# A transformer block with 64 experts: the last two tiles of tokens are handled apart behind the attention, and the last tile's rows go behind each expert's first 128 places

## The chip, the cores and the metric

One core of a Trainium2 chip runs the whole program in one launch. The metric is the time of the program on the device in microseconds (us). Times below come from one profiled execution unless they are called medians.

## The reference

All numbers are float32. 2 sequences of 512 tokens with 256 features (1024 tokens in all) go through attention and a layer of experts, each followed by a layer norm over the sum with its input:

```python
qkv = x @ Wqkv.T + b_qkv                     # 16 heads of 16
scores = einsum('bqhd,bkhd->bhqk', q, k) / 4 + alibi_bias; causal mask; p = softmax(scores)
x = layernorm(x + (p @ v) @ Wout.T + b_out)
...
probs = softmax(x @ gate_w.T)                # 64 experts
topk_w, topk_idx = top_k(probs, 8); topk_w /= topk_w.sum()
a = silu(x @ w1[e]) * (x @ w3[e])            # 256 -> 96
y = sum over the 8 chosen e of topk_w * (a @ w2[e])
x = layernorm(x + y)
```

Each token goes to 8 of 64 experts, so there are 8192 pairs of token and expert, 128 to an expert on average.

## The kernel before

**Attention.** The 1024 tokens are 8 tiles of 128 (4 to a sequence, numbered 0 to 3 by their query positions). They are worked on in four blocks of two tiles: `blocks_` lists sequence 0 tiles 0 and 1, sequence 0 tiles 2 and 3, sequence 1 tiles 2 and 3, sequence 1 tiles 0 and 1. A written-out loop goes over `step`; a step takes two heads. In it stand the scores of these heads (`scores`, L318 on PE, with the row's extreme on DVE, L324), the exponentials of the heads of three steps before (`exponentials`: products L369 on PE, Exp on ACT L379, and on POOL the triangle `affine_select` L384), and in every second step the products with the values (`values`, L406 on PE). A block takes 8 steps. The order on PE, DVE and ACT is the order in which the loop writes instructions. On POOL, selects and scatters are chained in order of issue by `in_order`.

**Small jobs.** When a block's last values are done, its remaining work is spread over the following steps, one job a step: `normalize` for each of its two tiles, `turn_context`, `project` (L455), `norm` with `turn_x1`, `route` (gate products L505, top 8 by L516 and L517), `weigh` (weights into columns of x1, L551) with `find_places` (L561 to L580: running counts `seen` by products with a triangle and with ones, then places). `find_places` gives every pair of token and expert a row in the table `xg` in HBM: expert e owns 288 rows from e*288, and the pair goes to the first free one.

**Scatters.** `dispatch` then issues 16 indirect DMAs on POOL for a block (L587), each of 128 rows of 329 floats, with `at(step + 8 + m // (8 if end else 1), dispatch, s, 2 * m, 2 * m + 2)`: two scatters a step from the eighth step on, and for the last block all at once.

**Experts.** After all 64 scatters (`after_scatters`), rows come back from `xg` by SP (L793) as 128-row jobs: 64 "one" jobs (an expert's first 128 places), 16 "four" jobs (places 128 to 159 of four experts, four DMAs), 8 "pair" jobs (two halves of 64 further places, found from the counts). The order is: a four, two ones, a pair every second time, two ones, and so on. A job turns the rows (L799 on PE, L801 on DVE), makes gate and up products (L810), Silu (L818), the weighted product (L820), turns it (L825, L827), makes the down product (L834), copies it to one of 10 buffers `y` (L842), and scatters it by POOL to `results` in HBM (L849). Rows are loaded 8 jobs ahead and more, into 18 buffers. Lists for all that (counts, places, which expert a row of a four belongs to) are worked out on DVE behind the last `find_places` (L697 to L787).

**Weights.** Two experts' weights are one DMA of 640 KB (L106). 9 pairs are loaded at the start, 10 during the attention, 4 behind it (`lates`), and the last 9 into the places of the first 9, each as soon as its two ones are done.

**The rare loop.** If the 288 places or the 8 pairs don't suffice, a loop (L899) of up to 64 turns handles what is left over, ahead of the jobs. With these inputs it makes no turn, but each engine loads its count (L896), branches and meets the others.

**End.** When all results are written, SP loads them (L995, 8 MB), PE and DVE add each token's 8 rows, and the last norm and the output follow.

Of the kernel before, what the change touches and what calls it, by code (L numbers as in the profile page):

```python
# [48 lines left out]
def block_kernel(ctx: ExitStack, tc: tile.TileContext, x, wqk, wv, bqk, slope, bv, wo, bo, gate, wall, out):  # L49
# [179 lines left out]
    with tc.tile_pool(name="ps_s", bufs=4, space=PSUM) as ps_s, tc.tile_pool(  # L229
# [5 lines left out]
        blocks_ = [(0, 0), (0, 1), (1, 1), (1, 0)]  # L235
# [67 lines left out]
        def maxima_of(s, g):  # L303
            h = blocks_[s][1]
            return maxima[h][(sum(other == h for _, other in blocks_[:s]) * NG + g) % 3]

        def scores(u, a):

            s, g, js = heads_of(u)
            b, h = blocks_[s]  # L310
            q = 2 * h + a
# [10 lines left out]
            for j, ps in zip(js, pss):  # L322
                junk = sm.tile([P, S], F32, tag="neg", name=f"neg{u}_{a}_{j}", bufs=2)
                nc.vector.tensor_tensor_reduce(  # L324
                    out=junk[:, :n],
                    in0=ps[:, :n],
                    in1=mask[:, S - n :],
                    scale=-1.0,
                    scalar=BIG,
                    op0=ALU.add,  # L330
                    op1=ALU.min,
                    accum_out=m[:, a, j * HP + HD + 1 : j * HP + HD + 2],
                )
# [3 lines left out]
        def lower(s, g):  # L337

            b, h = blocks_[s]
            m = maxima_of(s, g)  # L340
            pm = small
            for a in range(2):
                nc.tensor.transpose(pm[:, a * P : (a + 1) * P], m[:, a, :], ident)
            ql = sm.tile([P, W2], F32, tag="ql", name=f"ql{s}_{g}", bufs=3)
            nc.vector.tensor_tensor(ql, pm, qT[b][:, g, h * W2 : (h + 1) * W2], ALU.add)
# [4 lines left out]
        def parts_of(h):  # L350

            parts = []
            for k in range(0, 2 * h, 2):
                parts.append([(k, 0, 0), (k + 1, 0, W2)])
            parts.append([(2 * h, 0, 0), (2 * h + 1, P, W2)])
            return parts

        def exponentials(u, part):

            s, g, js = heads_of(u)  # L360
            b, h = blocks_[s]
            ql = lowered[s, g]
            todo = parts_of(h)[part]
            last = part == h
            pts = [ps_t.tile([P, S], F32, tag="pt", name=f"pt{u}_{part}_{n}") for n in range(2)]
            for k, first, col in todo:
                for n, j in enumerate(js):
                    r = slice(j * HP, (j + 1) * HP)
                    nc.tensor.matmul(  # L369
                        pts[n][:, col : col + W2 - first],  # L370
                        lhsT=kT[b][r, g, k * P : (k + 1) * P],
                        rhs=ql[r, first:],
# [3 lines left out]
            cols = W2 + P if last else S  # L376
# [21 lines left out]
        def values(s, g):  # L398
            b, h = blocks_[s]
            pc = halves[:, 0, :]  # L400
            u = s * NPAIR + 2 * g
            prs = [[probs.pop((u + j // 2, part, j % 2)) for part in range(h + 1)] for j in range(4)]
            for part, todo in enumerate(parts_of(h)):
                for k, first, col in todo:
                    for j in range(4):
# [3 lines left out]
                            rhs=prs[j][part][:, col : col + W2 - first],  # L409
                            start=(k == 0),  # L410
                            stop=(k == 2 * h + 1),
# [3 lines left out]
            nc.scalar.copy(raw[s][:, g, :], pc)  # L415
# [3 lines left out]
        def normalize(s, a):  # L419

            pm = ps_s.tile([P, S], F32, tag="ps", name=f"pcn{s}_{a}")
            for g in range(NG):
                nc.tensor.transpose(pm[:, g * P : (g + 1) * P], raw[s][:, g, a * P : (a + 1) * P], ident)
# [12 lines left out]
        def turn_context(s):  # L436
            pm = ps_s.tile([P, S], F32, tag="ps", name=f"pcT{s}")
            for a in range(2):
# [5 lines left out]
            nc.scalar.copy(ctxT[s].rearrange("p a d -> p (a d)"), pm)  # L444

        def first_of(s):
            b, h = blocks_[s]
            return b * NQ + 2 * h

        def project(s):  # L450
            i = first_of(s)
            pm = ps_s.tile([P, S], F32, tag="ps", name=f"po{s}")
            for a in range(2):
# [8 lines left out]
            mine = x1[:, i : i + 2, :D]  # L462
            nc.vector.tensor_tensor(mine, pm.rearrange("p (a d) -> p a d", d=D), mine, ALU.add)
            mv = means[s] = st.tile([P, 2, 2], F32, tag="mv", name=f"mv{s}")
            for a in range(2):
# [3 lines left out]
            roots[s] = st.tile([P, 2], F32, tag="rstd", name=f"rstd{s}")  # L469
            nc.scalar.activation(roots[s], mv[:, :, 1], AF.Sqrt, bias=eps_s)  # L470

        def norm(s):
            i = first_of(s)
            mv, r = means[s], roots[s]
            nc.vector.reciprocal(r, r)
            shift = st.tile([P, 2], F32, tag="shift", name=f"shift{s}")
            nc.vector.scalar_tensor_tensor(shift, mv[:, :, 0], -1.0, r, ALU.mult, ALU.mult)
            for a in range(2):
# [4 lines left out]
                x1_d[i * P : (i + 2) * P, :].rearrange("(n p) d -> p n d", p=P), x1[:, i : i + 2, :D]  # L483
            )

        def turn_x1(s):
            i = first_of(s)
            pm = ps_s.tile([P, S], F32, tag="ps", name=f"px1T{s}")
            for c in range(DC):
                for a in range(2):  # L490
                    nc.tensor.transpose(
                        pm[:, c * W2 + a * P : c * W2 + (a + 1) * P], x1[:, i + a, c * P : (c + 1) * P], ident
                    )
            x1Ts[s] = st.tile([P, DC, W2], F32, tag="x1T", name=f"x1T{s}", bufs=1)
            nc.scalar.copy(x1Ts[s].rearrange("p c q -> p (c q)"), pm)

        scatters = []

        masks, tos, expd = {}, {}, {}

        def route(s):
            pm = small[:, : 2 * E].rearrange("p (a e) -> p a e", e=E)
            for a in range(2):
# [10 lines left out]
            rest = st.tile([P, 2, E], F32, tag="rest", name=f"rest{s}")  # L514
            for a in range(2):
# [3 lines left out]
                )  # L519
            least = st.tile([P, 2], F32, tag="least", name=f"least{s}")  # L520
            nc.vector.tensor_scalar(least, top[:, :, 0], -1.0, None, ALU.mult)
            masks[s] = st.tile([P, 2, E], F32, tag="mk", name=f"mk{s}")
            nc.vector.tensor_scalar(masks[s], rest, -BIG, None, ALU.is_equal)
            lg = st.tile([P, 2, E], F32, tag="lg", name=f"lg{s}")
            den = st.tile([P, 2], F32, tag="den", name=f"den{s}")
            for a in range(2):
# [5 lines left out]
        def weigh(s):  # L532
            i = first_of(s)
            lg, den = expd.pop(s)
            nc.vector.reciprocal(den, den)
            rest = st.tile([P, 2, E], F32, tag="rest", name=f"chosen{s}")
            den2 = st.tile([P, 2], F32, tag="den2", name=f"den2{s}")
            for a in range(2):
# [13 lines left out]
                x1[:, i : i + 2, D : D + E], rest, den2.unsqueeze(2).to_broadcast([P, 2, E]), ALU.mult  # L552
            )

        def find_places(s):

            i = first_of(s)
            mk = masks.pop(s)
            pm = small[:, : 2 * E].rearrange("p (a e) -> p a e", e=E)
            for a in range(2):  # L560
                nc.tensor.matmul(pm[:, a, :], lhsT=ones, rhs=seen, start=True, stop=False)  # L561
                if a:
                    nc.tensor.matmul(pm[:, a, :], lhsT=ones, rhs=mk[:, 0, :], start=False, stop=False)
                nc.tensor.matmul(pm[:, a, :], lhsT=before, rhs=mk[:, a, :], start=False, stop=True)
            mine = nth[:, i : i + 2, :]
            nc.vector.tensor_copy(mine, pm)
            for a in range(2):
                nc.vector.tensor_tensor(seen, seen, mk[:, a, :], ALU.add)


            place = st.tile([P, 2, E], F32, tag="place", name=f"place{s}")
            nc.vector.tensor_scalar(place, mine, float(CAP), float(1 << 16), ALU.is_ge, ALU.mult)
            nc.vector.tensor_tensor(place, place, mine, ALU.add)
            nc.vector.tensor_tensor(place, place, begin.unsqueeze(1).to_broadcast([P, 2, E]), ALU.add)
            nc.vector.tensor_tensor(place, place, mk, ALU.mult)
            p8 = x1[:, i : i + 2, D + E : D + E + TOPK]
            for a in range(2):
                nc.vector.max(out=p8[:, a, :], in_=place[:, a, :])
            tos[s] = const.tile([P, 2, TOPK], I32, name=f"to{s}")
            nc.vector.scalar_tensor_tensor(tos[s], p8, -1.0, beyond[:, i : i + 2, :], ALU.add, ALU.min)  # L580

        def dispatch(s, first, end):
            b, h = blocks_[s]
# [496 lines left out]
```

## Time and profile before

| | us |
|---|---|
| median of 6 runs | 458.31 (456.12 to 459.12) |
| the profiled execution, its own time | 461.04 |
| its span, first to last instruction | 459.3 |

| engine | busy us | share of the span |
|---|---|---|
| PE (products) | 354.4 | 77% |
| DVE | 234.7 | 51% |
| POOL | 201.0 | 44% |
| ACT | 163.0 | 35% |

| when (us) | what |
|---|---|
| 0 to 204 | attention, with the small jobs and scatters of the first blocks in between |
| 204 to 255 | small jobs and scatters of the last block, the lists |
| 256 to 425 | the 88 jobs of the experts |
| 426 to 459 | results are loaded and added, last norm, output |

A line of the profile gives start and length, or length and busy times, then the engine (PEld is PE's weight load, SPq and POOLq are queues that issue DMAs), the line of the code, the operation, output and input, and in brackets how long the engine was idle before and what released it. "DMA share" is the mean busy share of the core's 16 DMA engines. The granted clock is that of PE, as a share of full speed.

### The profile page before, as it was taken

The page shows a single profiled execution, that of the slowest core. Times are in us where ns is not written, and L with a number is a line of the kernel's source. Part 1 is how long each engine was busy: PE and PEld are TensorE (multiplying, and loading weights), DVE is VectorE, ACT ScalarE, POOL GpSimd, SP SyncE. Part 2 cuts the span into 40 slices and gives each one's busy share as a digit, 9 for nine tenths or more (in the row PEclk, how much of TensorE's full clock was granted, in tenths as well). Part 3 has the DMA queues.
Part 4 walks back from the last instruction along what each step waited for, and adds up shares of the span by engine and source line. Part 5 has one row for each costly group of instructions (what it writes and reads, how often), then busy time and mean ns, then how long its engine had stood idle before and what let it go on. Part 6 is the DMA issues. An engine that isn't in the chain of part 4 may idle for free. (4 is left out here: it accounts for less than half of the span.)

```text
span 459.3 us, 8458 instructions
## 1 busy us (share of the span) xinstructions
PE 354.4 (77%) x2546; PEld 233.1 (51%) x2546; DVE 234.7 (51%) x1040; ACT 163.0 (35%) x453; POOL 201.0 (44%) x278
## 2 busy tenths in 40 slices
PE   4399999997999789775200397889898799997493
PEld 2135544665666556453200266556666566765372
DVE  0825445763676247243291255546565556653285
ACT  2012332565445533624010144434444444545032
POOL 8911112111165418647567044545554565656000
PEclk9769999995899679857555599999999999999599
DMA  8999999999542203314833489987786667211793
GB/s 246 391 360 332 324 316 328 320 266 358 195 133 75 83 0 120 111 60 147 297 123 128 122 273 329 294 274 229 244 256 212 208 182 217 70 68 57 319 408 108
DMA packets 56591, 98.58 MB, mean 215 GB/s; under 512 B 7241, under 2 KB 40600, under 8 KB 55520
## 3 DMA queue, kind: packets, MB, share of 16 engines
q1 hardware_dynamic: 47728, 76.93, 52.7%
q0 software_dynamic: 7456, 19.46, 11.9%
q10 hardware_dynamic: 1360, 1.64, 1.1%
q8 instruction: 21, 0.34, 0.3%
q14 instruction: 26, 0.21, 0.2%
HBM read 52.38 MB, written 48.75 MB: 220 GB/s over the span
## 5 line engine op out<-in xcount | busy, mean ns | idle before, releaser
L849 POOL DMA_INDIRECT results<-y,rows x88 | 86.6, 984 | 84.8 <-DVE xT L801 29.4
L324 DVE CUSTOM_DVE_ANT_0 neg<-ps,mask 128x256 f32<-128x256 f32 (+3 forms) x128 | 57.4, 487 | 44.4 <-PE ps L318 38.3
L587 POOL DMA_INDIRECT xg<-x,to x64 | 63.7, 996 | 22.2 <-issue 16.7
L384 POOL TENSOR_SCALAR_AFFINE_SELECT pr<-pr 128x256 f32<-128x256 f32 x64 | 25.0, 408 | 110.4 <-ACT pr L379 110.3
L379 ACT ACTIVATE pr<-pt 128x384 f32<-128x384 f32 (+1 forms) x96 | 45.3, 523 | 45.9 <-PE pt L369 37.4
L799 PE MATMUL pxT<-ident,xb 128*128 128x128 f32 x176 | 36.2, 287 | 29.6 <-SPq L941 29.2
L801 DVE COPY xT<-pxT 128x256 f32<-128x256 f32 x88 | 37.1, 422 | 35.5 <-DMA xb<-xg 17.0
L799 PEld LDWEIGHTS pxT<-ident,xb 128*128 128x128 f32 x176 | 23.0, 144 | 46.7 <-issue 39.6
L818 ACT ACTIVATE s<-pg 128x96 f32<-128x96 f32 x88 | 22.2, 253 | 62.5 <-PE pg L810 31.8
L842 ACT COPY y<-py 128x256 f32<-128x256 f32 x88 | 32.8, 373 | 20.5 <-PE pxT L799 11.0
L810 PE MATMUL pg<-w,xT 128*32 128x192 f32 (+1 forms) x288 | 39.9, 345 | 0.3 <-issue 0.3
L825 PE MATMUL paT<-ident,a 128*96 128x128 f32 x88 | 25.9, 294 | 14.9 <-DVE a L820 11.3
L273 PE MATMUL pq<-room 128*128 128x512 f32 x64 | 35.3, 687 | 0.1
L369 PE MATMUL pt<-ql,kT 32*128 32x256 f32 (+1 forms) x192 | 32.1, 410 | 1.5 <-ACT pr L379 1.0
L318 PE MATMUL ps<-room 32*128 32x128 f32 (+3 forms) x128 | 26.9, 496 | 7.6 <-DVE room L279 7.6
L318 PE MATMUL ps<-kT,qT 32*128 32x384 f32 (+3 forms) x128 | 30.5, 533 | 0.7 <-DVE maxima L324 0.7
L878 DVE CAST rows<-row 128x1 int32<-128x1 f32 x88 | 13.5, 154 | 34.0 <-DMA results<-y,rows 28.8
L810 PEld LDWEIGHTS pg<-w,xT 128*32 128x32 f32 (+1 forms) x288 | 27.9, 156 | 3.3 <-issue 1.5
L369 PE MATMUL pt<-ql,room 32*128 32x256 f32 (+1 forms) x192 | 28.0, 392 | 0.6 <-ACT pr L379 0.6
L834 PE MATMUL py<-w,aT 96*32 96x256 f32 (+1 forms) x144 | 27.9, 386 | 0.0
L827 ACT COPY aT<-paT 96x128 f32<-96x128 f32 x88 | 22.9, 260 | 11.8 <-PE paT L825 5.1
L369 PEld LDWEIGHTS pt<-ql,kT 32*128 32x128 f32 x192 | 21.4, 209 | 8.0 <-ACT pr L379 3.7
(200 smaller groups left out, 609.2 us busy)
## 6 DMA issues: line engine op xcount, KB each, us to landing
xg<-blank SPq DMA_DIRECT2D x8, 2632.0 KB
w<-in_wall_dram SPq DMA_DIRECT2D x18, 640.0 KB
xb<-xg SPq DMA_DIRECT2D x64, 164.5 KB
room<-in_wall_dram SPq DMA_DIRECT2D x10, 640.0 KB
room<-results SPq DMA_DIRECT2D x6, 1024.0 KB
wo<-in_wall_dram SPq DMA_DIRECT2D x16, 320.0 KB
xg<-blank SPq DMA_DIRECT2D x4, 658.0 KB
xb<-xg SPq DMA_DIRECT2D x64, 41.1 KB
```

The costliest lines, as they stand in the source:

```text
L273: nc.tensor.matmul(pq, lhsT=wqk_s[:, t, c, g * P : (g + 1) * P], rhs=xTs_[b][:, c, :], start=(c == 0), stop=(c == DC - 1))
L318: nc.tensor.matmul(ps[:, :n], lhsT=qT[b][r, g, q * P : (q + 1) * P], rhs=kT[b][r, g, :n], start=True, stop=True)
L324: nc.vector.tensor_tensor_reduce(out=junk[:, :n], in0=ps[:, :n], in1=mask[:, S - n :], scale=-1.0, scalar=BIG, op0=ALU.add, op1=ALU.min, a ...
L369: nc.tensor.matmul(pts[n][:, col : col + W2 - first], lhsT=kT[b][r, g, k * P : (k + 1) * P], rhs=ql[r, first:], start=True, stop=True,)
L379: nc.scalar.activation(pr[:, :cols], pts[n][:, :cols], AF.Exp, scale=SCALE)
L587: sc = nc.gpsimd.indirect_dma_start(out=xg[:, :], out_offset=bass.IndirectOffsetOnAxis(ap=tos[s][:, a, k : k + 1], axis=0), in_=x1[:, i + ...
L799: nc.tensor.transpose(pt[:, c * P : (c + 1) * P], xb[:, c * P : (c + 1) * P], ident)
L801: nc.vector.tensor_copy(xT, pt)
L810: nc.tensor.matmul(pg[r * m : (r + 1) * m, :], lhsT=xT[:, c * P + r * m : c * P + (r + 1) * m], rhs=w[:, c * 2 * I : (c + 1) * 2 * I], sta ...
L834: nc.tensor.matmul(py[r * m : (r + 1) * m, :], lhsT=aT[:I, r * m : (r + 1) * m], rhs=w[:I, DC * 2 * I :], start=True, stop=True,)
L842: nc.scalar.copy(y, py)
L849: a = nc.gpsimd.indirect_dma_start(out=results[:, :], out_offset=bass.IndirectOffsetOnAxis(ap=rows, axis=0), in_=y, in_offset=None, bounds ...
```

## The change

1. The blocks of the attention stay, but what follows them goes by `units`: the first three blocks as before, then the last block's two tiles as units 3 and 4, each with its own small jobs. Their jobs stand alternately, unit 3 first; unit 3 scatters 8 times, then unit 4 8 times.
2. The last tile (unit 4) takes its places behind `max(seen, 128)`: no row of it is among an expert's first 128 places. So the ones wait only for the scatters of the other seven tiles. Its counts come out of the same products as the total, so that `pcount` (L695) goes.
3. The third block's small jobs go two to a step, partly into the middle of a step (`HALF_STEPS`, `middle`). Scatters (`SCATTER`): the first block's two to a step as before, the second's four to a step, the third's four to a step from four steps behind the block's end on (before: two to a step from eight behind it).
4. `find_places` comes ahead of `weigh`.
5. The first 20 jobs are ones; then each of the 16 fours is followed by two or three ones, with a pair every second time. The last 9 pairs of weights are loaded when the four that uses the two pairs before them in place is done (two pairs after each of the first four fours, one after the fifth).
6. The rare loop goes behind the jobs and does all anew for what it handles; the list `left` (L780, L781) goes.

```diff
-        blocks_ = [(0, 0), (0, 1), (1, 1), (1, 0)]
+        blocks_ = [(0, 0, 2), (0, 2, 2), (1, 2, 2), (1, 0, 2)]
+        units = [(s, 0, 2) for s in range(len(blocks_) - 1)] + [(len(blocks_) - 1, a, 1) for a in range(2)]
...
+            if s < len(units) - 1:
...
+            else:
+                pm = room_for(s, 3)
+                nc.tensor.matmul(pm[:, 0, :], lhsT=ones, rhs=seen, start=True, stop=True)
+                nc.tensor.matmul(pm[:, 1, :], lhsT=before, rhs=mk[:, 0, :], start=True, stop=True)
+                nc.tensor.matmul(pm[:, 2, :], lhsT=ones, rhs=mk[:, 0, :], start=True, stop=True)
+                nc.vector.tensor_scalar(seen, pm[:, 0, :], float(P), None, ALU.max)
+                nc.vector.tensor_tensor(mine, pm[:, 1:2, :], seen.unsqueeze(1), ALU.add)
+                nc.vector.tensor_tensor(seen, pm[:, 2, :], seen, ALU.add)
...
+        HALF_STEPS = [[0, 2, 4, 6, 8, 10, 12], [0, 2, 4, 6, 8, 10, 12], [0, 1, 2, 3, 5, 7, 8], [0, 0, 2, 4, 6, 8, 10]]
+        SCATTER = [lambda k: 1 + k // 2, lambda k: 1 + k // 4, lambda k: k // 4, lambda k: 0]
...
-                        for m in range(8):
-                            at(step + 8 + m // (8 if end else 1), dispatch, s, 2 * m, 2 * m + 2)
+                        mine = [w for w, (of, _, _) in enumerate(units) if of == s]
+                        for w in mine:
...
+                            when = HALF_STEPS[s]
+                            for h, job in zip(when, todo_):
+                                for f, *args in job:
+                                    at(step + 1 + h // 2, f, *args, mid=h % 2 == 0 and s == 2)
+                            m = step + 1 + when[-1] // 2
+                            for k in range(0, nt * TOPK):
+                                at(m + SCATTER[s](k), dispatch, w, k, k + 1)
...
-                xb = load_places(n, [xg[k * CAP : k * CAP + P, :]])
+                xb = load_places(n, [xg[k * CAP : k * CAP + P, :]], own_block=True)
...
-        jobs = []
+        AT_FIRST = 20
+        jobs = [("one", e) for e in range(AT_FIRST)]
         for j in range(E // 4):
             jobs.append(("four", j))
-            jobs += [("one", e) for e in range(4 * j, 4 * j + 2)]
+            first, end = [AT_FIRST + (E - AT_FIRST) * m // (E // 4) for m in (j, j + 1)]
+            jobs += [("one", e) for e in range(first, end)]
             if j % 2 == 0:
-                jobs.append(("pair", j // 2))
-            jobs += [("one", e) for e in range(4 * j + 2, 4 * j + 4)]
+                jobs.insert(len(jobs) - 1, ("pair", j // 2))
...
-                    kind, e = jobs[n]
-                    pair = NOW + THEN + LATE + e // 2
-                    if kind == "one" and e % 2 and pair < E // 2:
-                        load_weights(pair, first_places[e // 2])
+                    kind, j = jobs[n]
+                    for pair in (2 * j, 2 * j + 1):
+                        if kind == "four" and NOW + THEN + LATE + pair < E // 2:
+                            load_weights(NOW + THEN + LATE + pair, first_places[pair])
```

The other edits carry the number of tiles of a unit (`nt`) through the helpers: the same operations on 128 columns instead of 256, products into other banks of the accumulator memory for single tiles (`room_for`).

## The prediction

> **What bounds the kernel now.** I read the slices of the page first, then the stretches, then POOL's instructions in order of time, then the chain of waits. In the slices (11.5 us each) PE is busy nearly everywhere except in the middle, slices 19 to 22.
>
> ```profile
> PE   4399999997999789775200397889898799997493
> PEclk9769999995899679857555599999999999999599
> DMA  8999999999542203314833489987786667211793
> ```
>
> The stretches (length, then busy time of PE, PEld, DVE, ACT, POOL with counts, granted clock, DMA share, GB/s) say who works there: PE for 0.79 us of 30, POOL for 17.43.
>
> ```profile
> 190.00:210.00 20.00, 15.29 (x84) 10.90 (x85) 6.08 (x30) 6.55 (x17) 11.10 (x15) 0.57 0.25 86
> 230.00:260.00 30.00, 0.79 (x4) 0.48 (x3) 12.75 (x57) 2.77 (x3) 17.43 (x19) 0.50 0.32 113
> 260.00:290.00 30.00, 26.82 (x202) 19.08 (x201) 17.09 (x90) 11.57 (x42) 11.83 (x12) 0.90 0.90 286
> 320.00:350.00 30.00, 26.87 (x216) 19.21 (x215) 17.52 (x93) 13.07 (x50) 15.84 (x18) 1.00 0.75 226
> 390.00:425.00 35.00, 30.66 (x232) 21.98 (x231) 18.96 (x99) 17.16 (x61) 21.65 (x22) 1.00 0.20 68
> ```
>
> POOL in order of time (start, length) shows a rhythm: a pair of triangle selects (L384) and two scatters (L587), back to back, 3.21 us a step of the attention; the last selects at 201.87; the last block's 16 scatters from 232.03 to 253.5.
>
> ```profile
> 173.16 0.77 POOL L384 TENSOR_SCALAR_AFFINE_SELECT pr<-pr 128x256 f32<-128x256 f32 x2
> 174.10 0.98 POOL L587 DMA_INDIRECT xg<-x,to  x1 [0.17 <-DVE maxima L324]
> 175.39 0.97 POOL L587 DMA_INDIRECT xg<-x,to  x1 [0.30 <-issue]
> 176.37 0.77 POOL L384 TENSOR_SCALAR_AFFINE_SELECT pr<-pr 128x256 f32<-128x256 f32 x2
> ...
> 201.87 0.78 POOL L384 TENSOR_SCALAR_AFFINE_SELECT pr<-pr 128x256 f32<-128x256 f32 x2 [3.85 <-ACT pr L379]
> ...
> 232.03 1.00 POOL L587 DMA_INDIRECT xg<-x,to  x1 [0.30 <-DVE blocks L704]
> 233.33 1.96 POOL L587 DMA_INDIRECT xg<-x,to  x1 [0.30 <-issue]
> ```
>
> The chain then runs from the last scatter through its landing and a load of rows to PE's expert work: the expert stage starts on the last scatter and on nothing else.
>
> ```profile
> 252.57 2.63 DMA xg<-x,to
> 256.30 0.35 SPq L793
> ...
> 258.17 2.45 DMA xb<-xg
> 260.66 0.69 PE pxT L799 x2
> ```
>
> **The sum, against the profiled execution** (461.04 us, its span 459.3; it is 2.7 above the median of 458.31).
>
> *Denser scatters, a cost.* The second block's 16 scatters go four to a step, not two, and the third block's go four to a step into the attention's last four steps instead of behind them. On POOL they stand in one queue with the selects, and PE, whose order is fixed, waits with its value products (L406) for the selects, and everything behind them on PE waits too. A step of POOL becomes 3.21 + 2 x 1.275 = 5.76 us (1.275 is the spacing of scatters). From 173.16 the fourth pair of selects starts at 190.5, the fifth at 196.2; they started at 182.8 and 186.0. The third block's scatters need places that PE computes behind the second value product, which needs the fourth selects: 191.3, then value product 0.9, scores 1.7, transposes 0.4 with a wait of 1, places 2.4, then on DVE places 2.4 and weights 1.4, is 201. Four scatters (5.1), selects (0.8), four scatters, selects: the last end at 213, and the last value product starts at 213.4, where it started at 204.09: **9.3 us later**. Bounds: 0 (PE keeps its own pace) and +10 (the same count with every scatter at once behind the other and 0.7 for a slower product). I take 9.3, since POOL had no gap at two scatters a step. The third block's scatters are then all out at 223.8 (226.4 before), so they hinder nobody.
>
> *The tail by single tiles.* From the last value product to the first scatter of that block it took 232.03 - 204.09 = 27.9. A hole is in it: PE's last place product ends at 223.27, DVE reads it at 228.89, while four 640 KB loads (L106) keep DMA at a share of 0.99. The trace names no releaser here.
>
> ```profile
> 228.89 0.29 DVE L566 COPY nth<-halves 128x128 f32<-128x128 f32 x1 [6.54 <-remote]
> ```
>
> Without the hole, 22.3. One tile instead of two halves the work on the way: projection (1.99) 1.0, routing product (1.97) 1.0, places (2.39) 1.3, transposes 1.5, statistics 0.6, top-8 0.5, scaling 0.5, in all -6.4. The weights now come behind the places: +1.4. On DVE the last tile's share and L755 (1.22) stand between: +2.5. List work no longer precedes the scatter on POOL: -0.6. That is 19.2, and the first scatter at 213.4 + 19.2 = 232.6. If the hole stays: 5.6 more.
>
> *Half as many scatters ahead of the first loads.* 7 x 1.275, and 2.63 for the landing: 244.2. By the waits in the program the first 20 loads wait for the first seven tiles' scatters alone. Load 0.1 + 2.45: PE starts at 247 where it started at 259.59: **-12.6**. The lists on DVE (229.7 to 243.3 before) lose L755, which now comes earlier, and L780/L781 (2.6 in all), gain the last tile's 17 small operations (2.5 by the neighbours' spacing), start some 2 us later and end near 245.5: just hidden, and where they end later each us counts. The last tile's scatters run on POOL until 253; results are written behind them there, and the first write came 8.2 us after PE's start (267.78), so at 255: hidden. The fours' loads wait for them on SP at job 20, some 30 us later: hidden.
>
> *Silu's table.* Its load (1.28 at 256.19, under the waiting for rows) now stands behind the first gate product: **+1.3**, with nothing beside it. In the trace a switch starts 0.02 us behind the copy ahead of it (209.42, 209.44), so 1.28 is all I count. The Trainium skill (ScalarE: Activation LUTs, What ACT_TABLE_LOAD costs) adds a drain of about 1.38 us to each switch; by it the sum would be 1.4 later.
>
> *The expert stage.* From 259.59 to the last write's end at 424.9 it took 165.3 for 88 jobs. Where no weights are reloaded (390 to 425) it does 22 jobs in 35 us, 1.59 each; 88 would take 140, with 8.2 of filling 148: 17 us are lost, mostly where DMA is 0.85 to 0.96 busy. Now the first 20 jobs have no reloads beside them, but all nine reloads (5.9 MB) come within five fours, 21 jobs: with rows, results and the pairs' weights some 13.4 MB, at the 285 GB/s of 260 to 290 it is 47 us where PE needs 35. Rows loaded ahead cover a part. I put 1 + 9 + 3 = 13 lost: **-4**; bounds -10 (hardly any lost behind the first jobs) and +4.
>
> *The rare loop at the end.* Its register loads, branches and barrier lay under the scatters; now they lie between the last write and the loads of results, and all queues wait. Behind the landing at 255.26 SP needed 1.04 to its next DMA, at the end now 0.14 (426.38 to 426.52): +0.9 at least. SP's own steps ahead of it (248.3 to 251.0, 2.7) may show: +3.6 at most. I take **+2.2**. The Sqrt table and the first products are pushed back with it, under the 4.7 us until a result is there (431.24).
>
> ```profile
> 423.95 0.98 POOL L849 DMA_INDIRECT results<-y,rows  x1 [0.30 <-issue]
> 426.52 2.95 SPq L995 DMA_DIRECT2D room<-results  x6
> ```
>
> Sum: -12.6 + 1.3 - 4 + 2.2 = -13.1, so 447.9 profiled, **445** at the median.
>
> The scatter at 233.33 took 1.96 instead of 0.97 while L755 ran on DVE. But L717 and L726, with two inputs in SBUF as well, left theirs at 0.97, so I add nothing to the sum and 1 us to the range. The GPSIMD Engine Reference (Specifications) speaks against denser scatters: POOL shares its SBUF interfaces with DVE operations of two SBUF inputs. If by it each of the seven scatters paid 0.98, the sum would be 7 us later.
>
> **The rivals.** *The hole stays* (20%): the late weights are still loaded beside the routing; 5.6 more, 450.6. *PE is not held by POOL* (17%): the last values come at 205, the single tile's scatters wait for POOL until 223.8 only; nearly 9 less, 436. Against it: POOL has no gap from 173 to 189. *The first loads still wait for all scatters* (3%), so the change doesn't do what it says: 8 x 1.275 = 10.2 more, 455; the program's waits speak against it. *Slower: the squeezed reloads* (10%). If those 13.4 MB run at 200 GB/s, it is 67 us, not 47; rows and weights come late, the stage loses 20, and the time is 465. It decides from some 215 GB/s down (62 us, all of the gain gone). 320 to 350 ran at 226, but at a DMA share of 0.75, not at a limit. The forecast keeps 50%.
>
> **How the numbers follow.** A difference under 0.3% (1.4 us) can't be told from none here. The range, 436 to 453, takes in the forecast with its bounds (-6 and +8 of the stage), the hole, and PE's free pace; the loads' waiting and the squeeze stay outside. Faster 0.87 (all but the squeeze and the loads' case), same 0.03, slower 0.10.
>
> **What would show it.** Right: selects 5.8 us apart from 173 on; the last values near 213; the single tile's first scatter near 233; PE's first expert product near 247 with POOL still scattering; a table load right ahead of the first Silu; reloads some 35 to 75 us into the stage with DMA at 0.9; 1 to 4 us between the last result's landing and the first load of results. Wrong: first loads of rows behind 253, or an expert stage of over 165 us.

## The result, and the profile after

The changed kernel takes 469.44 us at the median (464.72 to 473.41, 20 runs) where the kernel before, beside it, takes 458.19: a ratio of 1.022 (95% interval 1.019 to 1.024). It is slower; 445 was forecast. Of any kernel some executions take over 1.5% longer than its fastest: medians here are over all runs, ratios and their intervals leave the longer ones out, and the profiles of e1, e6, e10 and f1 below are of such longer ones. The profiled execution took 471.06 (span 469.3) against 461.04 (459.3), 10.0 more, and the trace splits this into three terms:

| term | before | after | difference | forecast |
|---|---|---|---|---|
| PE's first expert product | 259.59 | 262.54 | +3.0 | -12.6 |
| from there to the last write's end | 165.3 | 172.0 | +6.7 | -2.7 (Silu +1.3, order -4) |
| from there to the end | 34.4 | 34.8 | +0.4 | +2.2 |

The slices of the page of the changed kernel (PE's busy tenths and granted clock):

```profile
PE   4399999997998887582540598988789889997493
PEclk9679999996999598655755598999999999999598
```

PE's trough is not shorter: where slices 19 to 23 had 5, 2, 0, 0, 3 before, there is now 5, 8, 2, 5, 4, 0, 5 from slice 17 on, with the clock near a half. POOL in order of time (start, length, idle before it and who ended that) shows the start:

```profile
179.15 0.78 POOL L392 TENSOR_SCALAR_AFFINE_SELECT pr<-pr 128x256 f32<-128x256 f32 x2
...
184.92 0.77 POOL L392 TENSOR_SCALAR_AFFINE_SELECT pr<-pr 128x256 f32<-128x256 f32 x2
...
193.57 0.78 POOL L392 TENSOR_SCALAR_AFFINE_SELECT pr<-pr 128x256 f32<-128x256 f32 x2 [2.92 <-ACT pr L387]
...
212.32 0.98 POOL L619 DMA_INDIRECT xg<-x,to  x1 [6.21 <-DVE x L573]
...
217.12 0.78 POOL L392 TENSOR_SCALAR_AFFINE_SELECT pr<-pr 128x256 f32<-128x256 f32 x2
...
222.88 0.77 POOL L392 TENSOR_SCALAR_AFFINE_SELECT pr<-pr 128x256 f32<-128x256 f32 x2
...
246.95 0.98 POOL L619 DMA_INDIRECT xg<-x,to  x1 [12.97 <-issue]
```

The step from 179.15 to 184.92, 5.77 us, is the forecast's (5.76); the next pair of selects comes at 193.57, since POOL had to wait for ACT. The third block's first scatter is there only at 212.32, since its weights (L573) are late, and with seven others it stands ahead of the last two pairs of selects. So these come at 217.12 and 222.88 (201.87 before). DVE's timeline of the changed kernel has the next loss:

```profile
229.42 0.42 DVE L477 TENSOR_TENSOR x<-po,x 128x256 f32<-128x256 f32 x1 [1.52 <-issue]
233.92 0.23 DVE L761 TENSOR_SCALAR number<-number,half 128x8 f32<-128x8 f32 x1 [4.07 <-POOL number L760]
234.06 0.42 DVE L481 BATCH_NORM_STATS2 bn<-x 128x6 f32<-128x256 f32 x1
```

`number`, a small operation of the lists, stands in DVE's order between the single tile's projection and its statistics. It waits for POOL's iota (L760), and that waits in POOL's queue until 233.72, behind the third block's last scatters.

### The profile page after: what moved, and what is told of

Its sections match the earlier page's. It is cut to its first block, busy times and chain, and to the rows that moved or that the text cites. A ratio compares the mean times of both kernels' runs of the same rounds, so it can differ in the third digit from the quotient of the medians.

```text
span 469.3 us, 8469 instructions
## 1 busy us (share of the span) xinstructions
PE 362.7 (77%) x2544; PEld 237.6 (51%) x2544; DVE 234.3 (50%) x1055; ACT 161.6 (34%) x456; POOL 200.0 (43%) x277
## 3 DMA queue, kind: packets, MB, share of 16 engines
q0 software_dynamic: 7456, 19.46, 11.5%
## 5 line engine op out<-in xcount | busy, mean ns | idle before, releaser
L854 PEld LDWEIGHTS pg<-w,xT 128*32 128x32 f32 (+1 forms) x288 | 28.8, 157 | 2.6 <-issue 1.2
L878 PE MATMUL py<-w,aT 96*128 96x256 f32 (+1 forms) x144 | 28.8, 392 | 0.1
L871 ACT COPY aT<-paT 96x128 f32<-96x128 f32 x88 | 22.9, 260 | 16.6 <-PE paT L869 12.6
L869 PEld LDWEIGHTS paT<-ident,a 128*96 128x96 f32 x88 | 11.1, 126 | 33.4 <-DVE a L864 17.9
```

The lines of the kernel that those rows point to most:

```text
L854: nc.tensor.matmul(pg[r * m : (r + 1) * m, :], lhsT=xT[:, c * P + r * m : c * P + (r + 1) * m], rhs=w[:, c * 2 * I : (c + 1) * 2 * I], sta ...
L869: nc.tensor.transpose(pa[:I, :], a, ident)
```

## The experiments

The experiments ran on five chips. Before takes 463 us at the median on one of them, near the 458 of the result, and 444 to 448 on the other four; I call these the chips of 460 and of 444. Ratios are to before on the same chip. "Start" is PE's first expert product, "stage" runs from it to the last write's end, both from one profiled execution.

| run | chip | start | stage | median | ratio, 95% interval |
|---|---|---|---|---|---|
| a0_after | 444 | 255.6 | 162.0 | 452.95 | 1.018, 1.008 to 1.027 |
| b0_before | 444 | 252.6 | 157.4 | 445.92 (one) | |
| e1_spread | 444 | 247.5 | 160.6 | 442.33 | 0.993, 0.988 to 0.999 |
| e2_iota | 444 | 249.7 | 157.4 | 445.20 | 1.006, 1.001 to 1.011 |
| e3_order | 444 | 248.4 | 158.7 | 445.01 | 1.002, 0.996 to 1.008 |
| e6_behind_iota | 444 | 242.9 | 164.9 | 442.94 | 0.990, 0.984 to 0.996 |
| e7_rows | 444 | 248.6 | 154.1 | 440.42 | 0.991, 0.987 to 0.995 |
| e8_behind_rows | 444 | 241.9 | 152.6 | 430.18 | 0.969, 0.959 to 0.979 |
| e9_before_rows | 460 | 261.7 | 161.7 | 457.54 | 0.989, 0.980 to 0.998 |
| e10_order_rows | 460 | 263.8 | 164.2 | 461.54 | 0.997, 0.993 to 1.002 |
| e11_spread_reloads | 460 | 252.6 | 168.6 | 459.42 | 0.994, 0.990 to 0.998 |
| e12_iota_rows | 460 | 257.9 | 170.8 | 463.44 | 1.000, 0.995 to 1.005 |
| f1_behind_rows | 444 | 245.2 | 151.8 | 433.44 | (before 447.63) |
| f2_before_rows | 444 | 247.9 | 145.7 | 430.52 | 0.966, 0.954 to 0.979 |
| f3_spread_reloads | 444 | 240.5 | 148.9 | 428.09 | 0.964, 0.954 to 0.975 |
| f4_first8 | 444 | 241.9 | 154.2 | 434.68 | 0.978, 0.968 to 0.988 |
| g1_joined | 444 | 240.7 | 153.7 | 431.98 | 0.974, 0.969 to 0.978 |
| g2_before_rows | 444 | 251.0 | 144.8 | 432.55 | 0.976, 0.971 to 0.981 |

One chip ran e1, e2, e3 and e6, one a0, b0, e7 and e8, one e9 to e12, one f1 to f4, one g1 and g2. A start can differ by some 5 us between runs with the same front (e8, f1, f3), because they are apart already at 164 to 171 us, where the ninth last pair of selects stands. Counted from that pair, PE starts at 74.7 to 74.9 in e8, f1, f3, f4 and g1, and at 83.5 to 83.9 in e3, f2 and g2, so I give this count where starts are compared.

**The reference points.** a0 and b0 are the two kernels again, on one chip of 444.

> The changed kernel as it is, again, as the reference for the other runs of its chip (the chip of the first four runs ran the kernel before in 444 us, not 458). With the changed kernel's 1.022 of before: 454 on a chip where before takes 444; theory C (the iotas) then asks for about 1.015 or more, since without their wait it stood at 1.006 there.

> The kernel before as it is, for its profile on this chip. PE's first expert product about 248 if the chip is that of the first runs (the run with the changed order of jobs has the same front and started there), 259.6 if it is the first chip; PE's first product to the last write 157-159 in the first case, which would say that the order costs nothing, or 151-153, which would say that it costs some 6.

The change costs much the same here as in the result: start +3.0, stage +4.6, end +0.9.

**The start: scatters ahead of the selects.** e1 gives the second and third block their spacing of before:

```diff
-HALF_STEPS = [..., [0, 1, 2, 3, 5, 7, 8], ...]
+HALF_STEPS = [..., [0, 2, 4, 6, 8, 10, 12], ...]      # and mid=False
-SCATTER = [lambda k: 1 + k // 2, lambda k: 1 + k // 4, lambda k: k // 4, lambda k: 0]
+SCATTER = [lambda k: 1 + k // 2, lambda k: 1 + k // 2, lambda k: min(1 + k // 2, 6), lambda k: 0]
```

> The changed kernel with the second and third block's spacing of before: their scatters two to a step, the third block's small jobs one to a step, its scatters behind the attention; single tiles, order of jobs and loop stay as changed. (POOL's two iotas then stand ahead of the third block's scatters, so DVE's wait of 4.2 us for them goes as well.) Theory A (the third block's scatters and small jobs, put in front of the last selects, hold the last value product): the last selects fall back from 222.9 to 202-206, the last value product from 224 to about 205, the first single-tile scatter comes at 226-232 instead of 247, PE's first expert product at 241-247 instead of 262.5, and the time is 450-455 (-15 to -20). Rival B (the start is set by something else, such as the late weights' loads or the hole in PE's semaphores): PE starts at 255-262 and the time is 462-469.

The last selects came at 204.8 (216.6 in a0), the last value product ended at 208.5, and PE started at 247.5. Theory A's 241 to 247 was meant for a chip where the changed kernel starts at 262.5; here it starts at 255.6 (a0), and 8.1 us earlier (7.8 by the count) lie between theory A's 15 to 21 and the at most 7.5 of the rival. The ratio fell by 0.025, some 11 us, where theory A had 15 to 20. So the selects came back as theory A has it, and the start only in part. What sets it now is POOL: from 212.4 the 16 scatters of the third block and 8 of the first single tile go without a gap, 24 x 1.275 = 30.6.

e2 takes only DVE's wait away, e6 adds the third block's scatters behind the selects and leaves its dense small jobs:

```diff
+number0 = const.tile([P, NPS], F32, name="number0")    # e2: the same for quarter
+nc.gpsimd.iota(number0, pattern=[[2, NPS]], ...)       # with the constants at the start
-SCATTER = [..., lambda k: k // 4, lambda k: 0]         # e6 only
+SCATTER = [..., lambda k: 3 + k // 4, lambda k: 0]
```

> The changed kernel with POOL's two iotas (number, quarter) made with the other constants at the start, so that DVE's list work doesn't wait for POOL behind the third block's scatters. Theory C (DVE's stall from 229.84 to 234.06 lies on the path to the single tile's scatters): first single-tile scatter at 242.8 instead of 247.0, PE's first expert product at 258.3, time 465 (-4.2). Rival (something else is late next, such as the hole in PE's semaphores or POOL): within 1 us of the changed kernel, 468.5-470.

> The changed kernel with the iotas at the start, and the third block's 16 scatters three steps later, so that they all stand behind the attention's last selects; its small jobs stay dense. Theory A1 (the scatters in front of the last selects are the cost): last selects at 205-209 instead of 222.9, the third block's scatters run from about 213 to 233, the single tile's right behind them from 233 to 243.5, PE starts near 249, time 455-457. Theory A2 (the dense small jobs on PE, whose order is fixed, are the cost): last selects at 215-221, the scatters behind them until 241, the single tile's until 252, PE's start 257-259, time 463-466.

In e2 the statistics begin 0.46 us behind the beginning of the projection's sum (4.64 in the changed kernel), and POOL is idle for 7.8 us ahead of the single tile's first scatter (13.0 in a0): 5.2 less, where theory C asked for 4.2. The start stands 5.9 us ahead of a0's (9.9 by the count, of which 4.4 lies ahead of the third block's scatters, which the edit doesn't touch). The ratio is 0.012 under a0's, with intervals that overlap, on two chips of one kind. POOL's timeline of e2 (lines are 4 lower in these kernels):

```profile
205.63 0.98 POOL L623 DMA_INDIRECT xg<-x,to  x1 [6.22 <-DVE x L577]
...
210.46 0.77 POOL L396 TENSOR_SCALAR_AFFINE_SELECT pr<-pr 128x256 f32<-128x256 f32 x2
...
216.23 0.78 POOL L396 TENSOR_SCALAR_AFFINE_SELECT pr<-pr 128x256 f32<-128x256 f32 x2
```

and of e6, on the same chip:

```profile
205.56 0.79 POOL L396 TENSOR_SCALAR_AFFINE_SELECT pr<-pr 128x256 f32<-128x256 f32 x2 [2.23 <-ACT pr L391]
206.66 0.99 POOL L623 DMA_INDIRECT xg<-x,to  x1 [0.31 <-issue]
```

With the eight scatters out of their way the last selects come 10.7 us earlier, the moment their exponentials are there, and PE starts 6.8 us earlier (4.3 by the count); the ratio falls by 0.016. So it is the scatters ahead of the selects (A1). The dense small jobs (A2) cost the selects nothing: e6, which has them, is level with e1, which has not (205.6 and 204.8).

In these two profiles e6 ends its last write at 407.8 and e2 at 407.1, as if the stage had lost again what the start won. That isn't shown: e6's profiled execution is 1.4 us above its median and e2's 1.5 under, and by the ratios e6 is some 7 us quicker (2.3 at the medians), as much as the start won.

**The stage: the order of jobs.** e3 is the kernel before with the changed `jobs` and reloads alone.

> The kernel before with only the changed order of the experts' jobs and of the reloads (20 ones first, then sixteen fours with two reloads each behind the first fours). Theory D (the order costs the stage what was seen): PE's start unchanged at 259.6, stage from PE's first product to the last write's end 171-173 instead of 165.3, time 464-466 (+6 to +7). Rival E (the longer stage of the changed kernel comes from its later start, the 16 scatters on POOL or the clock, not the order): stage 164-167, time 457-460. Predicted in the forecast: -4, 454.

1.002, between 0.996 and 1.008, and a stage 1.2 longer than b0's (another chip of the kind): neither the +6 of theory D nor the -4 of the forecast.

**The stage: six buffers.** The waits of DVE in the stage of b0 (us in all, times, longest) name something that I had passed over in the trace of before, where it read 28.8 us in 24 times:

```profile
DVE rows L878 <- DMA results<-y,rows: 35.7, 34, 2.6
```

A job's row numbers are written as it begins and read by its scatter of results three jobs later. With 6 buffers, that scatter must have landed another three jobs later, 3 x 1.59 = 4.8 us; DVE waits if it has not, and with it PE, whose `paT` needs DVE. From a scatter to the rewriting of its buffer it took 4.2 us in the middle and up to 7.0 in the profile of before. All 24 waits there lie ahead of 390; from 390 to 425, where DMA's share is 0.20, there is none. e7 changes three numbers in the changed kernel:

```diff
-w  = work.tile([P, 1], F32, tag="rw",   ..., bufs=6)
+w  = work.tile([P, 1], F32, tag="rw",   ..., bufs=12)   # the same for tags row and rows
```

> The changed kernel with 12 buffers instead of 6 for the three small tiles of a job (weight, row, rows). A job's rows are read by its scatter of results, three jobs later, so with 6 buffers DVE waits for a scatter issued three jobs before to land (21.7 us in 14 waits in the expert stage of the changed kernel). Theory F (these landings hold the expert stage, and take back what an earlier start wins): those waits vanish, PE's waits of paT for DVE (11.2 us) fall under 5, the stage is 5-8 us shorter and the time 5-8 less. Rival G (DVE has slack there, and PE's own work and the clock set the stage): the waits vanish, the stage changes by less than 2 us, the time by less than 2.

The waits are gone, PE's wait for DVE is left with 0.3 us (9.8 in a0), and the time falls by 12.5 us. This is not the buffers' effect alone: the scheduler put `number` later in this kernel. That brings the start forward by 7.0, as in e2, and costs at the beginning of the stage, where DVE waits 11.5 us for the iota and PE 8.6 for DVE, so that the first write comes 16.9 us behind the start (9.1 in a0). From the first write to the last, where neither plays, it takes 136.3 us instead of 151.9.

> The third block's scatters behind the last selects, the iotas at the start, and 12 buffers for the small tiles. Theory F: the early start (242.9 in the run without the buffers, where the last write came at 406.8 all the same) now carries through: stage 156-158 instead of 163.9, time 6-8 less than without the buffers, about 436 on the chip of the first runs (0.98 of before). Rival G: 0.99 of before, as without the buffers.

This is 0.969 where e6, the same without the buffers, stood at 0.990, and 22.8 us less than the changed kernel on the same chip. Without the change at all, and with both kinds of chip:

> The kernel before with 12 buffers instead of 6 for the three small tiles of a job, nothing else. Theory F (landings of results behind 6 buffers hold the expert stage before the change as well; DVE waited 28.8 us for them in its profile, PE 11.3 for DVE): stage 148-152 instead of 156-157, time 5-8 less, 0.982-0.989 of before. The forecast's account (the 17 us lost in the stage are lost to the DMA traffic of rows and reloads itself): less than 2 us.

> The kernel before with 12 buffers for the small tiles, on this chip. On a chip of 444: theory F gives stage 149-151 instead of 156.5 and a ratio of 0.982-0.988, so the repaired change is worth 1.5% beyond the buffers. On a chip of 458-463: 0.989, as in the run before.

> The kernel before with 12 small buffers, beside the joined version on the same chip: 0.963-0.970 of before on a chip of 444, 0.985-0.992 on a chip of 458-463.

The kernel before gains 2.4 to 3.4% on the chips of 444 by the buffers alone (f2 more than theory F asked, g2 less than was then expected), and 1.1% on the chip of 460, with an interval from 0.2 to 2.0%. There DVE's waits for landings are gone as well, but PE still waits 9.2 us for DVE in e9 (11.3 in before), and the stage is 161.7. The stretch from 280 to 300 in b0 and in g2 (columns as in the stretches of before) shows that DMA was not what PE lacked:

```profile
280.00:300.00 20.00, 16.66 (x135) 12.31 (x132) 10.55 (x56) 8.78 (x31) 9.97 (x11) 1.00 0.93 298
```

```profile
280.00:300.00 20.00, 20.00 (x171) 14.93 (x170) 14.23 (x70) 10.32 (x39) 12.25 (x13) 1.00 1.02 342
```

PE is busy for the whole 20 us while DMA's share is 1.02. The stage of g2 is 144.8, with 1.57 a job from the first write to the last (136.4 for 87 jobs).

**The order again, with the buffers out of the way.**

> The kernel before with the changed order of jobs and reloads and with 12 buffers for the small tiles. The forecast's -4 for the order shows here if the landings alone hid it: stage 4 shorter and the time 3-5 less than with the buffers alone. Rival H (the two reloads behind each of the first fours fill the DMA, rows come late, and this takes back what the first 20 undisturbed jobs win): within 2 us of the run with the buffers alone, with the first 20 jobs 8-9 us faster and the next 21 to 45 slower by as much, PE waiting 3-8 us for rows (xb).

On the chip of 460 e10 is 4.0 us above e9 at the median (0.997 and 0.989, intervals that overlap), where the forecast had -4. Its stage is 2.5 longer, but its profiled execution is 2.3 above its median, e9's 1.8. Rival H isn't it: behind its start PE waits for no rows in e10. The ones are quicker (1.47 us from one `a` to the next, 1.60 in e9), the fours are slower (2.96, 2.32). ACT and PE around a four in e10:

```profile
392.59 0.86 PE L810 MATMUL pg<-w,xT 128*32 128x192 f32 x16
...
394.18 0.81 PE L810 MATMUL pg<-w,xT 128*128 128x192 f32 x4
395.28 0.25 ACT L818 ACTIVATE s<-pg 128x96 f32<-128x96 f32 x1 [2.44 <-PE pg L810]
```

The four's 16 gate products are over at 393.45 by the records, and its Silu begins at 395.28, when the next job's products are done as well. Over the 16 fours this delay is 0.95 us in the mean in the profile of before and 1.29 in that of after, 1.08 in e9, 1.76 in e10, and 0.07 in every run on the chips of 444. What makes it isn't settled; the ends of products are modelled, so PE may really be later there than its records say.

e11 and e8 differ in the reloads (and the chip), e12 and e11 in the reloads too and in the scatters ahead of the selects:

```diff
-for pair in (2 * j, 2 * j + 1):
-    if kind == "four" and NOW + THEN + LATE + pair < E // 2:
+pair = j                                                # e11, f3
+if kind == "four" and NOW + THEN + LATE + pair < E // 2:
```

> As the run of the third block's scatters behind the selects with 12 buffers, but one pair of weights reloaded behind each of the first nine fours instead of two behind each of the first five. Rival H (squeezed reloads are what is left: there DMA was at 1.00 from 290 to 310 and PE waited 6.4 us for rows from 310 to 330): these waits go, 3-6 us less, 424-427, 0.957-0.962 of before. Otherwise (the rows would be late anyway, or PE's clock sets the pace): within 1.5 us of 430, 0.969.

> The changed kernel with the iotas at the start and 12 buffers, the third block's first eight scatters in front of the last two pairs of selects as in the change. Theory A1: against the run with these scatters behind the selects (0.969 of before, PE's start 241.9), PE starts 6-8 us later (about 249) and, since the stage no longer takes it back, the time is 5-8 us more: 0.981-0.987 of before. Rival (the stage still ends by its own DMA traffic, whenever it starts): 0.967-0.973.

Both fell on the chip of 460, where e11 stands at 0.994 instead of 0.957 to 0.962 and can't be held against e8. e12 starts at 257.9, as theory C put it for this kind (258.3), e11 5.3 earlier. But 4.3 of these 5.3 they are apart at the ninth last selects already: by the count it is 1.0, though the last selects come 9.4 later in e12 by the same count, so on this chip it isn't shown that the scatters ahead of the selects cost the start what they do in e2 and e6. The medians are 4.0 us apart, with intervals that overlap. In both the stage takes 7 to 9 us more than e9's.

> The third block's scatters behind the selects, iotas at the start, 12 buffers, two reloads behind each of the first fours: the run that stood at 0.969 of before, on this chip. If this chip takes before in about 444: 0.965-0.973, fours' Silu 0.07 behind the last gate product. If it takes before in 458-463: 0.985-0.996, fours' Silu 1.5-1.8 late, PE's start 250-253, stage 166-168.

> As f1, with one reload behind each of the first nine fours. On a chip of 444: PE's waits for rows (6.4 us) go, 3-6 us less than f1. On a chip of 458-463, where the stage is slower than the reloads: within 2 us of f1.

> As f3 with 8 ones first instead of 20, so that the sixteen fours are spread over the other 80 jobs. Theory K (on the chips of 458-463 what the changed order costs the stage is paid at the fours, whose Silu starts 1.0 us behind the last gate product by the records in the order of before and 1.3-1.8 in the changed order; 0.07 on the chips of 444): on a slow chip the stage is 2-4 us shorter than f3's; on a fast chip the two are within 1.5 us. Rival L (the 8 scatters of the last tile, which the first four now waits for, hold SP and with it the rows behind): PE waits for rows near its 8th job, stage 3-6 us longer.

On one chip of 444: f3's stage is 3.0 shorter than f1's, f4's (8 ones first) 5.4 longer than f3's. What f3 wins over f1 in time isn't settled: f1's four runs are 426.16 and 432.88 to 434.23, f3's 425.90 to 431.66, and f1's profile (433.99, mean granted clock 0.852; f3's 0.877) is of a long one. Theory K asks for a chip of 460 and stays untested. For f1 PE's timeline shows where the squeezed reloads bite, behind a four, at a pair:

```profile
320.87 0.64 PE L880 MATMUL py<-room,aT 96*32 96x256 f32 x8
325.51 0.66 PE L845 MATMUL pxT<-ident,xb 128*128 128x128 f32 x2 [4.00 <-DMA xb<-xg]
```

It is PE's one long wait in that stage; e8, the same kernel, has one of 3.4 at that pair and one of 1.7 at a one. In f3 two of 1.7 and 1.9 are left, in f4 one of 3.5 at its first pair (job 11), after SP has waited 7.2 for the last tile's scatters (rival L), and 0.9 and 1.3 at later pairs. All but that 1.7 are for the rows of pairs, which f2, in the order of before, has with at most 1.2 us of waiting.

**All together.**

```diff
-AT_FIRST = 20
+AT_FIRST = 12          # beside e6's edits, 12 buffers, one reload a four
-AHEAD = 8
+AHEAD = 12
```

> Everything that the runs point to: the changed kernel with the iotas at the start, the third block's scatters behind the selects, 12 small buffers, one reload behind each of the first nine fours, 12 ones first, and rows loaded 12 jobs ahead instead of 8. On a chip of 444: start as in f3 (75 us behind the second block's first late selects), stage 145-147 instead of 148.0, time 422-428, 0.955-0.962 of before and 0.5-1.5% under the kernel before with the buffers alone. If the first four's rows hold SP until the last tile's scatters land (as with 8 ones first, where PE waited 3.5 us): stage 148-150 and no faster than the buffers alone. On a chip of 458-463: 0.985-0.993.

0.974 (expected: 0.955 to 0.962) against 0.976 for the buffers alone, the same; f3 and f2 stand alike too, 0.964 and 0.966. It starts 10.3 us earlier than g2, and its stage is 8.9 longer, with 6.0 us of waits for rows (most at pairs and one of 2.6 at a four, around which the granted clock is 0.86 for 10 us). So the change, mended, is worth nothing that shows; the version to take is the kernel before with 12 buffers, a change of three numbers. The changed order alone with 12 buffers wasn't run on a chip of 444, so what the order costs there isn't separated from the rest.

## Why the prediction was wrong, step by step

**Right.** POOL's step with four scatters (5.77, forecast 5.76), and PE held by POOL (the 17% rival is out). The tail: 23.3 from the last value product to the single tile's first scatter (223.7 to 246.95), of which 4.1 is DVE's wait for the iota, so 19.2 without it, as summed (the total; its parts weren't held against the trace one by one). The first loads go behind seven eighths of the scatters: at 259.21, while POOL issues the last tile's until 267. The Silu table: its load stands at 265.44 with 1.28, and in a0 the first Silu begins 1.38 behind its product. The Trainium skill (ScalarE: Activation LUTs, What ACT_TABLE_LOAD costs) would have 2.66 with the drain; the measured 1.38 decides, so no drain showed. Its rule on POOL's shared ports (GPSIMD Engine Reference, Specifications) was hardly put to the test: none of the denser scatters of the second and third block took over 1.05 us in the changed kernel (one took 1.79 in e6), but DVE stood idle beside eight of them, from 212 to 225.

**Failed: the third block's places at 201.** The items of the sum add to 201.5; the scatter that needs the places went at 212.3. The sum put the second value product right behind the fourth selects, at 191.3. These selects came 3.1 us late (193.57, forecast 190.5), and the product only 7.2 us behind their end, at 201.58:

```profile
194.42 1.39 PE L505 MATMUL px1T<-ident,x 128*128 128x128 f32 x4 [4.58 <-ACT x L493]
...
197.33 1.97 PE L526 MATMUL halves<-gate_s,x1T 128*128 128x64 f32 x8
...
201.58 1.51 PE L415 MATMUL halves<-pr,v 128*32 128x256 f32 x16 [1.12 <-ACT lg L548]
```

In PE's fixed order the block's transposes and routing product stood in front of it; PE waited 4.58 us for the norm on ACT, and the granted clock was 0.50 from 190.5 on. The sum had the chain behind the product and put what stands ahead of it at nothing. From the product to the scatter it took 10.7 us, forecast 9.7, and from there the eight scatters and two pairs of selects took the 11 to 12 us that were forecast. So the last value product ended its wait at 223.7, not 213.4: 10.3 of the 15.5 us that the start was missed by. That scatters in front of the last selects hold them is shown by e6 against e2. Why the product was late is read from the trace and stays open: it began 2.2 us behind the fourth selects in before, 7.5 in a0, but 3.0 in e2 with the same dense small jobs, and 6.9 in e1 with the spread ones.

**Failed: a wait overlooked.** The sum let the lists on DVE lie behind the last places, hidden, and put POOL's iotas at nothing. In the changed kernel the iotas stand behind the third block's last scatters; they hold DVE's `number`, and `number`, ahead of the statistics in DVE's order, holds these: 4.1 us, gone in e2. The -0.6 for list work that no longer stands ahead of the scatters on POOL has no counterpart: the iotas still stand there. The remaining 1.2 us is in the landing and the first load.

**Failed: the expert stage, -4.** Two errors. The first is the 17 us "lost where DMA is 0.85 to 0.96 busy". On the chips of 444 they were lost to the 6 buffers: the stage of the kernel before is 157.4 with 6 and 144.8 to 145.7 with 12, under the 148 that I gave an undisturbed one. Busy DMA was the circumstance: the waits for landings lie where it is busy. The Trainium skill (DMA: Bandwidth & Descriptors, Latency and other measured facts) has an HBM latency of 0.2 us on average and 2 us at high load; no run here times it alone. On the kind of chip that the forecast was read from, the buffers explain less: e9's stage is 161.7, only 3.6 under that of before's profile. From one `a` to the next its fours take 34.7 us in all, 26.1 in g2, its ones and pairs 118.4 (110.7), so the larger part of the 17 us stays open there. The order won nothing while the buffers stayed (e3), and nothing that shows with 12 of them (e10).

The second error is that the order has costs that I left out. On the chips of 460 these are the fours: their periods are 2.26 us in before and 2.66 in after, 16 x 0.4 = 6.4, where the +6.7 less Silu's 1.3 asks for 5.4; this is argued from the traces, not tried. On the chips of 444 they are rows of pairs behind bunched reloads, which show once the buffers don't bind (a wait of 3.4 us in e8, 4.0 in f1).

**The slower rival** (squeezed reloads, 10%) named a time near this one, but not this cause: in the changed kernel DMA was at 0.65 to 0.90 from 290 to 350. Its mechanism exists, in PE's waits for rows in e8 and f1; what it costs in time isn't settled.

**The loop at the end:** +0.4 in the result, +0.9 in a0 against b0, at or under the lower bound given (+0.9), not +2.2. The hole before 228.89 did not return.

Open: what delays a four's Silu on some chips and not on others, why pairs' rows in particular come late in the changed order, and why the second value product was late.

## What to carry to other kernels

Before pricing an earlier start, look for what paces the stage behind it, above all for a small tile with few buffers that an asynchronous transfer reads: its wait is one line in the view of waits, and it hides behind "DMA busy". In a queue that runs in order, list everything that a moved instruction gets in front of and who waits for each, constants' iotas included. A chain of small jobs across engines is priced by an instance of itself in the trace, not by the sum of its durations.

## What the runs showed of the hardware

The same program takes 444 to 448 us on four chips and 463 on a fifth, and an edit's worth differs with it (12 buffers: 2.4 to 3.4%, or 1.1%). On the fifth, and in the profiles of before and after beside the result, a Silu behind 16 gate products of 32 columns begins 1 to 1.8 us late by the records, on the four 0.07. And PE can run without a gap for 20 us while DMA moves 342 GB/s at a share of 1.02.
